# Four-layer graph stack on one core: row sums of layer two partly on VectorE, one more pair of lead in layer three

## The chip, the core and the metric

The kernel runs on one core of one Trainium2 chip. The metric is the device time of one execution in microseconds (us). PE is TensorE, DVE is VectorE, ACT is ScalarE, POOL is GpSimd, SP is the queue that issues most transfers. "L817" is line 817 of the kernel before; in the changed kernel the lines from there on are one lower or a few higher.

## The reference

There are 4096 nodes with 256 features each, and a dense 4096 x 4096 adjacency of zeros and ones. Four layers follow each other; each is attention over the whole graph, masked by the adjacency, then a residual and a layer norm:

```
x = layernorm(x + gat(x))          # layer 1: additive scores, 4 heads
x = layernorm(x + mha(x))          # layer 2: q, k, v with biases, 4 heads of 64
x = layernorm(x + gat1(x))         # layer 3: additive scores, 1 head
x = layernorm(x + cosine(x))       # layer 4: cosine scores

# layer 2
scores = q @ k.T / 8 + (edge.T - 1) * 10000;  ctx = softmax(scores) @ v
# layer 3
h = x @ W;  e = leaky(h @ a[:256] + (h @ a[256:]).T);  out = elu(softmax(where(adj > 0, e, -1e12)) @ h)
```

The sums behind the softmax of layer 2 (the "row sums") are needed for each query and head. Layer 3 needs two dot products for each row of x (source and destination scores). Both are what the change touches.

## The kernel before

All of x stays in SBUF as the tile `X`. Each layer is cut into 8 blocks (`NB`) of 512 query rows. PE, DVE and ACT run in the order in which the program is written ("manual schedule"); POOL and SP are placed by a planner, and each engine works through its own queue in order.

**Layer 2** (`multi_head_attention`). A block has 64 units (`NH`), one for each 64 key rows. Unit j does this:

- `scores`: 4 small products on PE into a PSUM tile `p` (L805), the exponential on ACT in place (L807). There are three buffers of `p`.
- `weights`: DVE multiplies `p` by the mask into `prob` (L817, 128 x 1024 elements). Then `prob` is added to the row sums `den`: for even j by a POOL tensor_tensor into part 0 of `den` (L824), for odd j by a DMA with accumulation that POOL issues, into part 1 or 2 (L830).
- `sums`: 4 products of V and `prob` on PE (L838), three units later (`LAG = 3`).

PE may write the scores of unit j + 3 only when DVE has multiplied unit j. Between the units, `finish(b - 1, j)` does the rest of the block before in small steps: join the parts of `den` (L847, j = 7 and 9), the outputs, the layer norm (L184, j = 35, 37, 39, 41), then `ga.dots` (L501, j = 43, 45, 47, 49), which makes the two dot products of 128 rows for layer 3, then `ga.factors` (j = 51), three exponentials and a small store. `finish` of step j comes after `weights` of unit j + 3, so the first dots follow the multiplication of unit 46.

A dot product is one DVE instruction (tensor_tensor_reduce, in the profile CUSTOM_DVE_ANT_0) that reads 256 elements of `X` and of `a_row`, both in SBUF, and a short one that reads the accumulator.

**Layer 3** (`additive_one`). A block has 16 pairs (`NP`) of 128 key rows. For pair g, `weights` loads a mask of 512 KB (L546, SP), ACT makes `r` (L553, two halves), DVE makes `prob` (L554, two halves) and the first half of `mix` (L434), POOL the second (L435, L436). `sums` does 7 products on PE (L444) two pairs later (`LAG = 2`); the tiles `prob` and `mix` have 3 buffers each, the mask 4. In block 0 there is no `mix`, and `sums` is 4 products (L568); the tail of layer 2 runs between them.

At the end of a block the four PSUM banks `acc` are emptied: `one` on ACT (L449), then five operations on DVE (L450 to L458). The next block's products write these banks. `finish(b - 1, g)` projects (L583, PE), divides and activates (`take`, L589 to L592), adds (`add`, L600, L601) and normalises the block before.

From block 2 on the block b - 2 is also prepared for layer 4 (`Cosine.preparing`, a generator that is moved on one step at chosen g): DVE transposes `y` into `squares` (L127), SP writes `squares` to DRAM (`far`, L131) and reads it back turned (`xT`, L135); then 8 products (L1033), two PSUM banks, with 8 squares on ACT (L1037) written between them; a root (L1040, L159, L160); POOL refines it (L166 to L169); ACT scales (`rows`, L1046); DVE transposes `rows` into a second tile `squares`, POOL writes it to DRAM and reads it back. The two tiles `squares` come from two pools of one buffer each: `gb_squares` and `co_once`.

## Time and profile before

| | us |
|---|---|
| median of 3 runs (lowest to highest) | 2887.21 (2884.02 to 2887.65) |
| the profiled execution, its own time | 2885.52 |
| its span in the profile | 2883.7 |
| TensorE busy in the span | 2798.0 (97%) |
| VectorE, ScalarE, GpSimd busy | 2307.1, 1698.3, 1118.9 |
| granted TensorE clock, mean | 0.997 |

The span is 1.8 us shorter than the execution's own time, and that is 1.7 us under the median. The products of layer 1 end at 724 us of the span, layer 2 runs its units from 812 to 1758 us, layer 3 from there to about 2242 us, layer 4 to the end. In the views below, an instruction's line gives its start, its duration, engine, source line, operation and tiles; in brackets stands the idle time ahead of it and what ended that. A line of waits gives the waiting engine and tile, what it waited for, the total, the number of times and the longest.

### The profile page before, as it was taken

The page shows a single profiled execution, that of the slowest core. Times are in us where ns is not written, and L with a number is a line of the kernel's source. Part 1 is how long each engine was busy: PE and PEld are TensorE (multiplying, and loading weights), DVE is VectorE, ACT ScalarE, POOL GpSimd, SP SyncE. Part 2 cuts the span into 40 slices and gives each one's busy share as a digit, 9 for nine tenths or more (in the row PEclk, how much of TensorE's full clock was granted, in tenths as well). Part 3 has the DMA queues.
Part 4 walks back from the last instruction along what each step waited for, and adds up shares of the span by engine and source line. Part 5 has one row for each costly group of instructions (what it writes and reads, how often), then busy time and mean ns, then how long its engine had stood idle before and what let it go on. Part 6 is the DMA issues. An engine that isn't in the chain of part 4 may idle for free. (4 is left out here: it accounts for less than half of the span.)

```text
span 2883.7 us, 50258 instructions
## 1 busy us (share of the span) xinstructions
PE 2798.0 (97%) x19489; PEld 1427.6 (50%) x19489; DVE 2307.1 (80%) x3010; ACT 1698.3 (59%) x2641; POOL 1118.9 (39%) x1009
## 2 busy tenths in 40 slices
PE   9999999999999999999999998999999999999998
PEld 4333333333543333333333333777877777777776
DVE  8899999998767888788887888777777766666666
ACT  7899999997256655656556564555555422222222
POOL 0010010100068988888888883344445100000000
PEclk9999999999999999999999999999999999999999
DMA  7566667665259989988888987566567544444441
GB/s 207 103 140 138 141 137 148 136 132 92 88 125 193 184 175 161 193 177 180 176 164 187 181 178 178 161 193 199 173 179 212 131 63 63 62 63 60 65 55 34
DMA packets 243666, 405.38 MB, mean 141 GB/s; under 512 B 25201, under 2 KB 125537, under 8 KB 242530
## 3 DMA queue, kind: packets, MB, share of 16 engines
q0 software_dynamic: 103648, 182.48, 40.6%
q1 hardware_dynamic: 133264, 212.45, 24.3%
q10 hardware_dynamic: 6514, 7.23, 0.7%
q8 instruction: 153, 2.51, 0.4%
q14 instruction: 87, 0.71, 0.1%
HBM read 332.27 MB, written 35.73 MB: 128 GB/s over the span
## 5 line engine op out<-in xcount | busy, mean ns | idle before, releaser
L807 ACT ACTIVATE p<-p,shift 128x1024 f32<-128x1024 f32 x512 | 556.2, 1088 | 356.8 <-PE p L805 349.5
L817 DVE TENSOR_TENSOR prob<-p,mask 128x1024 f32<-128x1024 f32 x512 | 620.3, 1221 | 171.7 <-ACT p L807 160.9
L310 PE MATMUL acc<-prob,V 128*32 128x512 f32 x6144 | 664.0, 593 | 1.2 <-DVE prob L300 1.2
L824 POOL TENSOR_TENSOR den<-den,prob 128x1024 f32<-128x1024 f32 x248 | 635.9, 2564 | 51.2 <-DVE prob L817 41.4
L297 ACT ACTIVATE prob<-row,dst 128x512 f32<-128x512 f32 x1020 | 635.0, 712 | 0.6
L300 DVE SCALAR_TENSOR_TENSOR prob<-prob,mask 128x2048 f32<-128x2048 f32 x256 | 580.5, 2287 | 25.7 <-ACT prob L297 25.1
L805 PE MATMUL p<-qT,kT 64*64 64x512 f32 x4096 | 538.7, 592 | 39.6 <-DVE prob L817 39.6
L838 PE MATMUL acc<-prob,V 64*64 64x512 f32 x4096 | 536.8, 589 | 0.0
L310 PEld LDWEIGHTS acc<-prob,V 128*32 128x32 f32 x6144 | 197.3, 110 | 453.0 <-issue 431.6
L444 PE MATMUL acc<-mix,mixed 128*128 128x256 f32 x1440 | 391.4, 381 | 5.7 <-POOL mix L435 4.7
L805 PEld LDWEIGHTS p<-qT,kT 64*64 64x64 f32 x4096 | 153.1, 133 | 325.5 <-issue 237.6
L838 PEld LDWEIGHTS acc<-prob,V 64*64 64x64 f32 x4096 | 157.5, 133 | 285.7 <-issue 278.2
L444 PEld LDWEIGHTS acc<-mix,mixed 128*128 128x128 f32 x1440 | 272.2, 190 | 48.1 <-POOL mix L435 7.9
L1096 DVE TENSOR_TENSOR prob<-prob,mask 128x1024 f32<-128x1024 f32 x128 | 156.5, 1222 | 169.8 <-ACT prob L1088 169.6
L90 POOL COPY tick<-prob 128x1 f32<-128x1 f32 x35 | 38.9, 1112 | 643.3 <-DVE prob L300 642.4
L830 POOL DMA_DIRECT2D den<-prob x240 | 232.7, 969 | 81.4 <-DVE prob L817 59.9
L554 DVE SCALAR_TENSOR_TENSOR prob<-r,own,mask 128x512 f32<-128x512 f32 x256 | 179.7, 743 | 103.7 <-POOL mix L436 42.6
L444 PE MATMUL acc<-prob,X 128*128 128x256 f32 x960 | 251.2, 381 | 10.8 <-DVE quarters L450 9.0
L1021 POOL DMA_DIRECT2D mask<-in_adjT x64 | 47.8, 746 | 521.4 <-DVE prob L1096 418.7
L444 PEld LDWEIGHTS acc<-prob,X 128*128 128x128 f32 x960 | 181.0, 190 | 96.5 <-issue 63.1
L1088 ACT ACTIVATE prob<-p 128x512 f32<-128x512 f32 x144 | 86.0, 598 | 220.8 <-PE p L1084 204.4
L1088 ACT ACTIVATE prob<-g 128x512 f32<-128x512 f32 x112 | 66.7, 596 | 195.5 <-PE g L1084 195.5
(211 smaller groups left out, 2838.3 us busy)
## 6 DMA issues: line engine op xcount, KB each, us to landing
mask<-in_adjT SPq DMA_DIRECT2D x256, 512.0 KB
den<-prob POOLq DMA_DIRECT2D x240, 512.0 KB, 5.3
mask<-edges SPq DMA_DIRECT2D x512, 64.0 KB
mask<-in_adjT POOLq DMA_DIRECT2D x64, 512.0 KB, 5.6
edges<-in_adj POOLq DMA_DIRECT2D x32, 512.0 KB, 9.8
far<-squares SPq DMA_DIRECT2D x16, 512.0 KB
den<-prob SPq DMA_DIRECT2D x16, 512.0 KB
row<-far SPq DMA_DIRECT2D x7, 1024.0 KB
```

The lines of the kernel that those rows point to most:

```text
L297: nc.scalar.activation(z[:, h, :], r, AF.Relu, bias=-1.0, scale=dst[:, j, h:h + 1])
L300: nc.vector.scalar_tensor_tensor(z, z, 1.0, mask[m][:, j % MJ, :].unsqueeze(1).to_broadcast([P, H, QW]), OP.add, OP.mult)
L310: nc.tensor.matmul(acc[b][h * G:(h + 1) * G, n, :], part, prob[b, j][:, h, :], start=(j == 0), stop=(j == NT - 1))
L444: nc.tensor.matmul(acc[at][:, half * HW:(half + 1) * HW], w, a, start=(g == 0 and half == 0), stop=(g == NP - 1), skip_group_check=True)
L554: nc.vector.scalar_tensor_tensor(z[:, n, :], r, ga.own[:, j:j + 1], mask[:, n, :], OP.add, OP.mult)
L805: nc.tensor.matmul(p[c * d:(c + 1) * d, r, :], kT[half, c, at:at + d], qT[half, c, cols], start=True, stop=True)
L807: nc.scalar.activation(p, p, AF.Exp, bias=shift)
L817: nc.vector.tensor_tensor(z, p, mask[m][:, j % MJ, :].unsqueeze(1).to_broadcast([P, KC, QW]), OP.mult)
L824: nc.gpsimd.tensor_tensor(to, to, flat, OP.add)
L830: nc.gpsimd.dma_start(to, flat, accum_op=OP.add)
L838: nc.tensor.matmul(acc[b][c][r * d:(r + 1) * d, :], V[half, j, r * d:(r + 1) * d], prob[b, j][half, r, :], start=(j == 0), stop=(j == NH - 1))
L1096: nc.vector.tensor_tensor(z, z, co.mask[b, 2 * g // MJ][:, lo:lo + 2, :], OP.mult)
```

## The change

Layer 2: in the blocks 1 to 7, the additions of units 44, 48, 52 and 56 to part 0 of `den` go from POOL to DVE (28 of 248 POOL additions). The dots move to the steps right behind these, so that DVE's order there is multiplication, addition, two dot products. `factors` moves from step 51 to 57, the load of the first row for layer 3 from step 57 of block 0 to step 63 of block 1.

Layer 3: `LAG` goes from 2 to 3, `prob` and `mix` get 4 buffers, the mask 3. The first `squares` shares the one buffer of the second. `finish` and the preparation are laid out anew over g; in the preparation the 8 products come first, and the 8 squares follow in two later steps.

Layer 4 takes the two added steps of the preparation up in its own list.

```diff
@@ additive_one
-            mp = pool(lay, "gb_mask", 4)
-            zp = pool(lay, "gb_z", 3)
+            mp = pool(lay, "gb_mask", 3)
+            zp = pool(lay, "gb_z", 4)
...
-            sq = pool(lay, "gb_squares", 1)
             far = pool(lay, "gb_far", 2, space=bass.MemoryType.DRAM)
-            follow.turning = xp, sq, far
+            follow.turning = xp, None, far
...
             def finish(b, g):
+                if g in (1, 3, 5, 7):
+                    project(bank, b, g // 2)
                 if g in (2, 4, 6, 8):
-                    project(bank, b, g // 2 - 1)
+                    take(sb, b, g // 2 - 1)
                 if g in (3, 5, 7, 9):
-                    take(sb, b, g // 2 - 1)
-                if g in (4, 6, 8, 10):
-                    add(b, g // 2 - 2)
+                    add(b, g // 2 - 1)
+                elif g == 10:
+                    roots[b] = begin_root(mvs[b])
                 elif g == 11:
-                    roots[b] = begin_root(mvs[b])
-                elif g == 12:
                     v, r, n = roots[b]
                     end_root(v, r, n, nc.gpsimd)
...
-                elif g in (13, 14):
+                elif g in (12, 13):
                     v, r, _ = roots[b]
-                    for k in (2 * g - 26, 2 * g - 25):
+                    for k in (2 * g - 24, 2 * g - 23):
...
-                elif g == 15:
+                elif g == 14:
...
-            LAG = 2
+            LAG = 3
...
-                        if b > 1 and g in (3, 5, 10, 11, 12, 13, 14, 15):
+                        if b > 1 and g in (0, 2, 8, 9, 10, 11, 12, 13, 14, 15):
                             follow.prepare(bank, b - 2, 1)
@@ multi_head_attention, weights
                     else:
-                        nc.gpsimd.tensor_tensor(to, to, flat, OP.add)
+                        eng = nc.vector if b and j in relief else nc.gpsimd
+                        eng.tensor_tensor(to, to, flat, OP.add)
@@ multi_head_attention, finish
-                elif j in (43, 45, 47, 49):
-                    ga.dots(b * QB + (j - 43) // 2)
-                elif j == 51:
+                if j + LAG in relief:
+                    ga.dots(b * QB + relief.index(j + LAG))
+                elif j == 57:
                     ga.factors(b)
-                elif j == 57 and b == 0:
-                    ga.row(b, nc.sync)
+                elif j == 63 and b == 1:
+                    ga.row(0, nc.sync)
...
             LAG = 3
+            relief = (44, 48, 52, 56)
@@ Cosine.preparing
-            xT = yield from block_turning(*self.turning, rows, nc.sync)
+            turned, squares, far = self.turning
+            xT = yield from block_turning(turned, squares or self.once, far, rows, nc.sync)
...
                     nc.tensor.matmul(prs[k // 2][:, k % 2, :, :], xT[:, c, k], w_sb[:, c, :],
                                      start=(c == 0), stop=(c == KC - 1))
+            for k in range(QB):
+                if k % 2 == 0:
+                    yield
                 for n in range(2):
                     sq = in_.tile([P, P], FP, name="sq")
                     nc.scalar.activation(sq, prs[k // 2][:, k % 2, n, :], AF.Square, accum_out=norm[:, k, n:n + 1])
@@ cosine_attention
-            steps = {(0, j + n): (NB - 2 + b, step) for b, j in enumerate((1, 12)) for n, step in ((0, 3), (4, 1), (5, 1), (7, 1), (8, 3))}
+            steps = {(0, j + n): (NB - 2 + b, step) for b, j in enumerate((1, 12)) for n, step in ((0, 3), (4, 3), (5, 1), (7, 1), (8, 3))}
```

## The prediction

> **What bounds the kernel now.** I read the busy shares first: PE is busy for 97% of the span, and the mean granted clock is 0.997. A change that moves no PE work can only win back the idle time of PE, so I next asked what PE waits for in layer 2 (window 825 to 1745) and layer 3 (1745 to 2250).

> ```profile
> PE 2798.0 (97%) x19489; PEld 1427.6 (50%) x19489; DVE 2307.1 (80%) x3010; ACT 1698.3 (59%) x2641; POOL 1118.9 (39%) x1009
> ...
> PE p L805 <- DVE prob L817: 38.8, 28, 2.0
> ...
> PE g L1033 <- ACT sq L1037: 9.3, 12, 1.1
> PE acc L444 <- DVE quarters L450: 9.0, 6, 1.7
> PE acc L444 <- POOL mix L435: 4.7, 8, 0.8
> ```

> The second line is all that PE loses in layer 2: 28 waits, which is 7 blocks of 4. The others belong to layer 3. The timeline around the first dots of block 1 (DVE, then POOL, then PE) shows where the 28 come from, and the last two lines show the same dots later, in layer 3:

> ```profile
> 1004.93 1.23 DVE L817 TENSOR_TENSOR prob<-p,mask 128x1024 f32<-128x1024 f32 x1 [0.56 <-ACT p L807]
> 1006.07 0.42 DVE L501 CUSTOM_DVE_ANT_0 neg<-X,a_row 128x256 f32<-128x256 f32 x1
> 1006.41 0.08 DVE L501 DVE_READ_ACCUMULATOR2_ANT dot<- 128x1 f32 x1
> 1006.53 2.73 DVE L501 CUSTOM_DVE_ANT_0 neg<-X,a_row 128x256 f32<-128x256 f32 x1
> 1009.19 0.08 DVE L501 DVE_READ_ACCUMULATOR2_ANT dot<- 128x1 f32 x1
> 1009.19 2.35 DVE L817 TENSOR_TENSOR prob<-p,mask 128x1024 f32<-128x1024 f32 x2
> ...
> 1006.31 2.66 POOL L824 TENSOR_TENSOR den<-den,prob 128x1024 f32<-128x1024 f32 x1
> ...
> 1010.46 1.09 PE L805 MATMUL p<-qT,kT 64*64 64x512 f32 x8 [0.78 <-DVE prob L817]
> ...
> 1015.56 1.09 PE L805 MATMUL p<-qT,kT 64*64 64x512 f32 x8 [1.44 <-DVE prob L817]
> ...
> 1791.50 0.43 DVE L501 CUSTOM_DVE_ANT_0 neg<-X,a_row 128x256 f32<-128x256 f32 x1
> 1791.97 0.42 DVE L501 CUSTOM_DVE_ANT_0 neg<-X,a_row 128x256 f32<-128x256 f32 x1
> ```

> The first dot takes 0.42. Then POOL starts its addition (1006.31 to 1008.97), and the second dot takes 2.73 and ends with it. In layer 3, where POOL adds nothing, all eight dots take 0.42 or 0.43. A dot costs 0.42 alone and lasts until POOL is done beside an addition.

> **Layer 2: what is removed.** PE starts units 1.72 us apart. The product after the first dots starts at 1010.46 instead of 1009.50, 0.96 late; each of the next three comes 1.62 late (DVE takes 5.10 for two units that PE makes in 3.43). A block loses 0.96 + 3 x 1.62 = 5.82, seven blocks 40.7 us.

> **Layer 2: what is added.** I take slack from the same place. Normally DVE has 0.56 of idle time per unit. Between multiplications 46 and 47 stood 3.12 us of dots, so DVE came 3.12 - 0.56 = 2.56 late and PE 0.96: some 1.6 us of lateness is free. Now DVE's insert at unit 48 is the addition, 1.14 from start to start (the nearest row is L847, the same form, 1216 ns in each of 14 executions, beside busy POOL), and two dots with their reads, 0.46 each: 2.06. That is 1.50 late, nothing lost. But the addition reads `den`, so it must wait for POOL's addition of unit 46. POOL starts 0.28 after the multiplication of 46 and takes 2.35; DVE, catching up, has multiplied 48 only 2.35 after 46. That makes a wait of about 0.35, a lateness of 1.85, a loss of 0.25. At unit 44 a scaled row (L184, 0.34) joins: 0.25 to 0.5. A block loses 1.0 to 1.2, seven blocks 7.7 us. Bounds: nothing, if POOL always keeps up; 15 us, twice that, since POOL's additions beside transfers reach 3.1 (block 5 runs 0.9 behind). Net for layer 2: -33 (-41 to -26).

> Everything queued behind the waiting addition on DVE is the two dots and multiplication 45, 49 and so on; PE waits for that, which is what I priced. POOL's next addition (46, 50) waits for DVE's, but also for a later multiplication, so costs nothing. POOL is freed of 28 x 2.56 = 72 us; its idle time there is not on the path. `factors` moves to where no dot is queued before it (ACT waited 1.6 us for the last dot), and the row load moves along SP with half a layer in hand: both nothing.

> [...]

> **Layer 3.** Per block, PE's waits between 2061.85 and 2124.30 are 0.71 + 0.77 (products behind squares on the same banks), 0.78 (`mix`) and 0.37 + 1.69 + 0.20 at the end, where DVE is late:

> ```profile
> 2121.34 1.40 DVE L554 SCALAR_TENSOR_TENSOR prob<-r,own,mask 128x512 f32<-128x512 f32 x2
> 2122.78 0.87 DVE L434 TENSOR_TENSOR mix<-prob 128x512 f32<-128x512 f32 x1
> 2123.57 0.68 DVE L450 TENSOR_TENSOR quarters<-one,acc 128x512 f32<-128x512 f32 x1
> ...
> 2121.91 0.70 PE L444 MATMUL acc<-prob,X 128*128 128x256 f32 x2 [0.37 <-ACT one L449]
> 2124.30 0.70 PE L444 MATMUL acc<-prob,X 128*128 128x256 f32 x2 [1.69 <-DVE quarters L450]
> ```

> With the products ahead of the squares, the 1.48 go. The third pair of lead covers the 0.78. But the end gets later. I follow DVE from the pair after the last `take` (pair 12, DVE at 2099.93 before) to the emptying of the banks. Before, it takes 23.6 us (L450 at 2123.57). After, I add the rows up: pair 13 at +4.0 (no squares ahead of it); 14 at +8.5, since ACT must do one root (0.35) and four squares (1.1) before `r`; 15 at +12.1; 16 at +16.6, behind eight scalings (2.17); the transposes of `rows`; 17 at +19.9. Then comes the new wait: the transpose of `y` needs the shared `squares`, which POOL still writes to DRAM. POOL issues that after `mix` of pair 16, at about +20.2, and before it took 3.7 (2119.82 to 2123.5), so the transpose starts at +23.9, 2 us late; pair 18 follows at +25.2, L450 at +27.2. Queued behind it on DVE are pair 18 and the emptying, and PE waits for the latter. The transpose, though, stood behind the emptying before, so that pair 3 of the next block comes at +29.7 in both. From there to the next pair 12 it is 31.5 after (take and add pairs, 7.85 for two) and 32.7 before. A block takes about 61.2 instead of 61.4 to 62.4: -0.7 each for five blocks, -3.5. The last block has neither the shared tile's wait nor a block behind it and keeps its 1.88 + 0.70: -2.6. At the start, the joins of the row sums go behind a fourth pair, whose mask is issued only after the first pair (1762.84): +1.5, between 0 and 3. In the middle of a block a mask has two pairs (6 us) to land; the nearest row, POOL's mask, lands in 5.6, so nothing. Net: -4. Bounds: the chain after pair 12 may be all hidden (five blocks of 1.48 + 0.78 + 1.3, where 1.3 is 2.26 less the 0.96 that the undisturbed end of block 1 costs, and the last block: -20), or the transfer lands 2 to 3 us later than in my row (five times: +12).

> **Sum.** Against the profiled execution: 2885.5 - 33 - 4 = 2848.5. That execution is 1.7 under the median of the runs, so I say 2850.

> **Rivals.** (1) Layer 3 comes clean: the lead hides the shared tile. For it: POOL's transfer could land sooner. Against: the wait stands ahead of the emptying in DVE's order. Time: 2885.5 - 33 - 20 + 1.7 = 2834. (2) Layer 3 loses: the same wait, longer, since transfers are busy there (0.65 of the engines). Time: 2885.5 - 33 + 12 + 1.7 = 2866. (3) Slower: POOL lags behind DVE by a pair, and each moved addition waits for it. POOL is nearly full in layer 2 (45 of 50 us), and an addition with its issue takes 2.56 + 0.97. A wait of 3.5 makes 2.06 + 3.5 - 0.56 - 1.6 = 3.4 lost at each of 28, 95 us in all: 2885.5 - 40.7 + 95 - 4 + 1.7 = 2937. It decides from a wait of some 1.7 us on: (40.7 + 4) / 28 = 1.6 lost at each, and 0.1 that the slack takes. Against: POOL starts that addition 0.15 to 0.6 us after its multiplication in six blocks, 0.96 in block 5. (4) The change doesn't do what it says: the dots still last 2.45 for another reason, such as POOL's issues. Then 2.0 more is lost at each, 28 x 2.0 = 56: 2885.5 - 40.7 + 56 - 4 + 1.7 = 2898. Against: one dot beside an issue alone took 0.61.

> **How the numbers follow.** My forecast has 0.57, rival 1 0.15, rival 2 0.20, rivals 3 and 4 together 0.04; 0.04 is for gain and loss cancelling, within 0.2% (5.8 us, about what this kernel's measurement can tell from none). So faster 0.92, same 0.04, slower 0.04. The range goes from rival 1 to rival 2 with the bounds of layer 2 partly added: 2832 to 2869.

> **What would show it.** In layer 2: all dots at 0.42, PE's wait for L817 from 38.8 to under 15, blocks of about 114.6 us instead of 119.3 (the first scores of block 1 start at 920.74, of block 7 at 1636.40). In layer 3: no wait of PE for the squares or `mix`, a DVE wait for a POOL transfer ahead of L127, PE's wait for L450 grown to some 4 us per block. Dots of over 1 us, or additions on DVE preceded by over 1.5 us of idle time, would prove me wrong.

## The result and the profile after

| us | before | after |
|---|---|---|
| median of 16 runs on one chip | 2886.84 | 2893.90 |
| lowest to highest | 2884.02 to 2890.03 | 2886.74 to 2901.31 |
| the profiled execution (its span) | 2885.52 (2883.7) | 2892.32 (2890.5) |
| mean granted TensorE clock | 0.997 | 0.987 |

One run of after (5999.05 us) was disturbed as a whole and is left out of the range; the median of the other 15 is 2893.70. The ratio of after to before is 1.0026, 95% interval 1.0018 to 1.0034: the changed kernel is 0.26% **slower**. The forecast was 2850 (2832 to 2869), so it missed by 44 us, and its sign was wrong.

First the page of after, its span and busy shares:

```profile
span 2890.5 us, 50162 instructions
PE 2803.9 (97%) x19489; PEld 1440.2 (50%) x19489; DVE 2276.5 (79%) x3038; ACT 1694.1 (59%) x2641; POOL 1049.3 (36%) x981
```

DVE and POOL have less to do, as meant, but PE is busy for 6 us longer with the same 19489 products: some of them ran at a lower clock (mean granted 0.987 instead of 0.997). The waits of PE in layer 2 (window 825 to 1745; a line that belongs to layer 3 is left out) show that the stated aim was reached, and that something else came in:

```profile
...
PE acc L838 <- ACT kept L843: 6.8, 4, 2.9
PE p L804 <- DVE prob L816: 3.2, 5, 1.1
PE acc L838 <- issue: 2.1, 1, 2.1
```

The 38.8 us of waits for the multiplication are down to 3.2. New are waits for `kept` (the copy of a finished block's sums out of PSUM), at the changeover from one block to the next. The waits of PE in layer 3 (window 1720 to 2260):

```profile
PE acc L444 <- DVE quarters L450: 37.0, 6, 8.1
PE acc L567 <- DVE prob L553: 8.5, 1, 8.5
PE g L1035 <- ACT h L591: 4.4, 6, 1.0
PE g L860 <- DVE den L847: 2.2, 1, 2.2
```

The waits for the squares (9.3) and for `mix` (4.7) are gone; the wait for the emptying went from 9.0 to 37.0.

I cut the span at four instants that both traces have: first and last scores of layer 2 (L804), the emptying (L450) of block 1 of layer 3, of block 6, of block 7. The same cuts serve for all experiments.

| us of the span | before | after | difference | forecast |
|---|---|---|---|---|
| layer 2, first to last scores | 942.3 | 915.5 | -26.8 | -33 |
| start of layer 3, to the emptying of block 1 | 122.2 | 133.0 | +10.8 | +1.5 |
| blocks 2 to 6 of layer 3 | 308.1 | 332.0 | +23.9 | -3.5 |
| last block of layer 3 | 58.2 | 56.9 | -1.3 | -2.6 |
| everything else | 1452.9 | 1453.1 | +0.2 | 0 |

So the gain of layer 2 came (a fifth short) and layer 3 took it away, and more. Three places had to be explained: the 6 us short in layer 2, the 9 us too many at the start of layer 3, and the 27 us in its blocks.

**The blocks of layer 3.** DVE, then PE, at the end of block 5 in the trace of after (start, duration, engine, line, operation, tiles, in brackets the idle time ahead and what ended it):

```profile
2050.16 1.30 DVE L127 STREAM_TRANSPOSE squares<-rows 128x512 f32<-128x512 f32 x2
2051.38 1.37 DVE L553 SCALAR_TENSOR_TENSOR prob<-r,own,mask 128x512 f32<-128x512 f32 x2
...
2057.16 1.30 DVE L127 STREAM_TRANSPOSE squares<-y 128x512 f32<-128x512 f32 x2 [3.69 <-DMA far<-squares]
2058.39 1.37 DVE L553 SCALAR_TENSOR_TENSOR prob<-r,own,mask 128x512 f32<-128x512 f32 x2
...
2060.40 0.68 DVE L450 TENSOR_TENSOR quarters<-one,acc 128x512 f32<-128x512 f32 x1
```

```profile
2053.97 0.70 PE L444 MATMUL acc<-prob,X 128*128 128x256 f32 x2 [0.69 <-ACT one L449]
2061.14 1.22 PE L444 MATMUL acc<-prob,X 128*128 128x256 f32 x2 [6.47 <-DVE quarters L450]
2062.16 1.91 PE L444 MATMUL acc<-mix,mixed 128*128 128x256 f32 x4
2063.86 1.06 PE L444 MATMUL acc<-mix,X 128*128 128x256 f32 x2
...
2069.04 0.59 PE L444 MATMUL acc<-mix,mixed 128*128 128x256 f32 x2
```

The transposition of `y` waits 3.69 for POOL's transfer out of the one `squares` tile; a pair and the emptying stand behind it, so PE idles 6.47. And then the products take 1.06 for 0.59: after this wait the records show a granted clock of 0.50 from 2057.1 to 2067.3. The same follows each of the six block ends, for 3.4, 10.2, 6.8, 10.2, 6.8 and 6.8 us. The first of these, of block 1, where POOL has no transfer out of `squares` under way yet, stands behind a wait of 2.57 us; the others stand behind waits of 6.5 to 8.1.

**The end of layer 2.** The waits for `kept` led to a place where no instruction is busy. This is the view of the transfers of after from 1376 to 1390, in 40 slices of 0.35 us: the busy tenths of the 16 DMA engines, GB/s, and one queue's packets, MB and share:

```profile
DMA  6999900000359999794000002866498999999999
GB/s 151 164 253 221 211 13 0 0 0 0 6 97 165 148 94 39 12 35 12 0 0 0 0 0 41 64 61 82 101 192 178 218 218 212 263 203 237 243 282 209
...
q10 hardware_dynamic: 528, 0.00, 2.1%
```

Queue 10 is the store of `factors` (`far<-src`, L514): 512 pieces of 4 bytes, issued at 1374.1 and moved at 1376.3 to 1376.7. Hardly anything is moved from 1377.8 to 1379.8 and from 1381.3 to 1384.4. Packet by packet, 4 KB pieces of the additions to `den` that take 0.33 us otherwise then take up to 5.25. In layer 2 such packets (4 KB or less, over 1 us) come in one bunch per block, apart from a few single ones; each bunch begins 1.7 to 4.2 us behind the first of this store's packets, in before and after alike (122 and 150 of the 30,720 packets of 4 KB). The change moved the store, with `factors`, from step 51 to 57, that is from unit 54 to unit 60 of the block. Before, the last packet of the last bunch ended at 1749.6, and the first masks of layer 3 were issued at 1755.3. After, the packets of that bunch start from 1729.0 to 1736.6, and the masks are issued at 1728.4. DVE at the start of layer 3 in after:

```profile
1739.44 1.41 DVE L553 SCALAR_TENSOR_TENSOR prob<-r,own,mask 128x512 f32<-128x512 f32 x2 [6.80 <-DMA mask<-in_adjT]
...
1747.15 1.41 DVE L553 SCALAR_TENSOR_TENSOR prob<-r,own,mask 128x512 f32<-128x512 f32 x2 [4.66 <-DMA mask<-in_adjT]
```

The first mask is used 11.1 us after its issue; before it was 6.1 (1755.32 to 1761.41).

### The profile page after: what moved, and what is told of

Its sections match the earlier page's. It is cut to its first block, busy times and chain, and to the rows that moved or that the text cites. A ratio compares the mean times of both kernels' runs of the same rounds, so it can differ in the third digit from the quotient of the medians.

```text
span 2890.5 us, 50162 instructions
## 1 busy us (share of the span) xinstructions
PE 2803.9 (97%) x19489; PEld 1440.2 (50%) x19489; DVE 2276.5 (79%) x3038; ACT 1694.1 (59%) x2641; POOL 1049.3 (36%) x981
## 5 line engine op out<-in xcount | busy, mean ns | idle before, releaser
L300 DVE SCALAR_TENSOR_TENSOR prob<-prob,mask 128x2048 f32<-128x2048 f32 x256 | 580.3, 2285 | 25.8 <-ACT prob L297 25.2
L824 POOL TENSOR_TENSOR den<-den,prob 128x1024 f32<-128x1024 f32 x220 | 560.9, 2549 | 41.2 <-DVE prob L816 33.0
L804 PE MATMUL p<-qT,kT 64*64 64x512 f32 x4096 | 535.0, 592 | 4.7 <-DVE prob L816 4.0
L444 PE MATMUL acc<-mix,mixed 128*128 128x256 f32 x1440 | 395.7, 384 | 0.7 <-DVE quarters L577 0.7
L444 PEld LDWEIGHTS acc<-mix,mixed 128*128 128x128 f32 x1440 | 277.4, 193 | 40.1 <-issue 1.0
L804 PEld LDWEIGHTS p<-qT,kT 64*64 64x64 f32 x4096 | 152.9, 133 | 287.1 <-issue 233.7
L444 PE MATMUL acc<-prob,X 128*128 128x256 f32 x960 | 253.9, 384 | 38.9 <-DVE quarters L450 37.0
L830 POOL DMA_DIRECT2D den<-prob x240 | 228.0, 950 | 137.6 <-DVE prob L816 92.9
L444 PEld LDWEIGHTS acc<-prob,X 128*128 128x128 f32 x960 | 182.7, 192 | 125.2 <-issue 63.1
```

The costliest lines, as they stand in the source:

```text
L300: nc.vector.scalar_tensor_tensor(z, z, 1.0, mask[m][:, j % MJ, :].unsqueeze(1).to_broadcast([P, H, QW]), OP.add, OP.mult)
L444: nc.tensor.matmul(acc[at][:, half * HW:(half + 1) * HW], w, a, start=(g == 0 and half == 0), stop=(g == NP - 1), skip_group_check=True)
L804: nc.tensor.matmul(p[c * d:(c + 1) * d, r, :], kT[half, c, at:at + d], qT[half, c, cols], start=True, stop=True)
L824: eng.tensor_tensor(to, to, flat, OP.add)
L830: nc.gpsimd.dma_start(to, flat, accum_op=OP.add)
```

## The experiments

Every ratio is to the kernel before, run beside it. The last four columns are the cuts of the table above. Line numbers in a view are those of the run's own kernel, and the code of the edits is abridged.

| run | median, us | ratio (95% interval) | layer 2 | start | blocks 2 to 6 | last |
|---|---|---|---|---|---|---|
| before (profile) | | | 942.3 | 122.2 | 308.1 | 58.2 |
| after (profile) | 2893.90 | 1.0026 (1.0018 to 1.0034) | 915.5 | 133.0 | 332.0 | 56.9 |
| l2_only | 2868.44 | 0.9928 (0.9913 to 0.9943) | 924.2 | 128.2 | 308.0 | 57.8 |
| l3_only | 2914.51 | 1.0087 (1.0072 to 1.0102) | 944.2 | 129.1 | 328.0 | 57.1 |
| turn_late | 2875.55 | 0.9950 (0.9936 to 0.9965) | 920.9 | 133.2 | 307.9 | 60.0 |
| own_squares | 2872.47 | 0.9950 (0.9933 to 0.9966) | 918.6 | 133.4 | 308.2 | 56.8 |
| l2_odd | 2894.40 | 1.0032 (1.0022 to 1.0041) | 945.5 | 126.6 | 308.5 | 58.0 |
| own_squares_odd | 2900.82 | 1.0052 (1.0037 to 1.0067) | 947.7 | 131.6 | 307.7 | 56.8 |
| l2_products_first | 2857.26 | 0.9901 (0.9886 to 0.9916) | 914.4 | 128.0 | 303.1 | 56.3 |
| l2_odd_products_first | 2885.92 | 0.9999 (0.9990 to 1.0008) | 948.4 | 126.2 | 300.8 | 57.4 |
| l2_store_late | 2883.71 | 0.9995 (0.9986 to 1.0004) | 936.6 | 127.5 | 307.6 | 57.8 |
| l2_early | 2852.66 | 0.9882 (0.9866 to 0.9899) | 907.5 | 125.2 | 308.9 | 59.4 |
| l2_early_products_first | 2844.51 | 0.9858 (0.9843 to 0.9872) | 907.2 | 125.8 | 301.1 | 56.6 |
| after_early | 2873.97 | 0.9960 (0.9945 to 0.9975) | 906.6 | 127.6 | 328.7 | 57.3 |
| after_wide_store | 2868.33 | 0.9934 (0.9919 to 0.9949) | 900.5 | 126.1 | 330.4 | 56.5 |
| after_early_own | 2854.90 | 0.9884 (0.9868 to 0.9901) | 907.2 | 128.4 | 307.6 | 56.9 |
| turned_store | 2839.32 | 0.9836 (0.9819 to 0.9852) | 905.5 | 120.9 | 301.9 | 56.3 |
| turned_store_sp | 2835.29 | 0.9819 (0.9805 to 0.9834) | 901.0 | 123.8 | 300.8 | 56.3 |

The theory at this point: layer 2's part is a gain of some 27 us, the layer-3 part loses some 24 us by the shared `squares`, and the slow start of layer 3 comes from layer 2's transfers. The rivals: the longer lead itself is the loss, or the two parts only hurt together.

### The two halves of the change, each alone

l2_only is the kernel before with the edits of `multi_head_attention` alone; l3_only is after without them.

> The kernel before with the layer-2 part of the change alone (additions of units 44, 48, 52, 56 on VectorE, dots behind them). My theory (layer 2 gains 27 us as in the trace of after, and the 10.8 us that the start of layer 3 lost come from this part, since the transfers that accumulate den lag at the end of the faster layer 2): time 11 to 18 us below before, first mask of layer 3 again some 11 us after its issue. Rival A (the start of layer 3 lost its 10.8 us to the three mask buffers and the fourth pair of lead): 24 to 29 us below before, first mask some 6 us after its issue.

> The kernel after with the layer-2 part undone, so the layer-3 part alone. My theory: the blocks 2 to 6 of layer 3 lose some 24 us, the last gains 1.3, the start is nearly unchanged: 20 to 26 us above before. Rival A (the start's loss belongs to this part): 31 to 36 us above before. Rival B (the two parts hurt each other, neither does alone): within 5 us of before.

The parts are nearly additive: -0.72% and +0.87%, together +0.15%, against +0.26% measured. l3_only lies 25.6 us above before (20 to 26 expected), l2_only 20.5 below, between what theory and rival said. At the start of layer 3 both were half right: l2_only loses 6.0 there, l3_only 6.9.

### The shared squares

```
turn_late:    elif g == 14: ... far_y store
-                 follow.prepare(bank, b, 1, ys[b])
+             elif g == 15: follow.prepare(bank, b, 1, ys[b])
own_squares:  sq = pool(lay, "gb_squares", 1); follow.turning = xp, sq, far
              co_mask bufs=4 -> 3
```

> The kernel after with the transposition of y moved from step 14 back behind the emptying of the banks (step 15), still into the shared buffer. My theory (the wait for the shared squares, and the half clock after PE's long wait, are paid because the transposition stands ahead of the emptying in VectorE's order): PE's wait for the emptying falls from 6.2 to 2 to 3 us a block, the half clock goes, blocks 2 to 6 from 66.3 to about 62 us: 18 to 24 us below after. Rival (the longer lead itself makes the chain to the emptying long, with a pair more ahead of it): the wait stays above 5 us, time within 6 us of after.

> The kernel after with a buffer of its own for the first squares, paid with one of the four mask buffers of layer 4 (4 to 3). The transposition stays ahead of the emptying, but waits for no transfer. My theory: the wait of 3.7 us goes, PE's wait for the emptying falls from 6.2 to about 2.5 to 3.5 us a block (the transposition itself, 2.6, stays ahead of the emptying), blocks 2 to 6 at 62 to 63 us: 15 to 22 us below after, unless layer 4 pays for its third mask buffer. Rival (it is the order and the lead, not the shared buffer): the wait stays above 5 us and the time within 6 us of after.

Both give blocks 2 to 6 their old 308 us back: 24 us for an edit of place, 24 for a buffer. DVE, then PE, at the same block end in own_squares:

```profile
2046.73 1.30 DVE L127 STREAM_TRANSPOSE squares<-y 128x512 f32<-128x512 f32 x2
...
2049.96 0.68 DVE L450 TENSOR_TENSOR quarters<-one,acc 128x512 f32<-128x512 f32 x1
```

```profile
2050.70 1.22 PE L444 MATMUL acc<-prob,X 128*128 128x256 f32 x2 [2.70 <-DVE quarters L450]
```

The same order and the same lead, but no wait ahead of the transposition: PE idles 2.70 instead of 6.47. The rival falls; by the ratios both are 0.76% (22 us) below after. But neither is better than before in these blocks. What the waits for squares and `mix` gave back, new ones take: PE waits 16.1 us for the emptying in own_squares (9.0 before), and 12.6 us for `h` in turn_late. In own_squares the granted clock is still 0.50 for 3.4 us behind each of the six block ends.

### A wrong turn: fewer transfers

At this point I took the transfers of `den` themselves for the reason of the late block ends (the engines are busy to 0.92 in layer 2), and gave POOL four of them per block to add.

```
-                    if j < 4:
+                    if b and j - 1 in relief:
+                        nc.gpsimd.tensor_tensor(den[b][:, 0, :], den[b][:, 0, :], flat, OP.add)
+                    elif j < 4:
```

> The layer-2 part alone, and GpSimd, which it freed of four additions a block, adds the units 45, 49, 53 and 57 of blocks 1 to 7 itself, in place of 28 of the 224 accumulating transfers of these blocks. My theory (the faster layer 2 now meets the transfers of den: VectorE's multiplication waits for a transfer that still reads its prob buffer, 17 to 25 us in all, and the first masks of layer 3 queue behind them): these waits fall under 8 us, PE's waits for kept (10.1 us) under 4, layer 2 from 924 to 912 to 917 us, the first mask of layer 3 lands in 6 to 9 us instead of 12: time 8 to 15 us below the layer-2 part alone. Rival (the limit is not the transfers but the order on VectorE and ScalarE at the end of a block): layer 2 within 3 us of 924, PE's waits for kept stay.

> The kernel after with its own squares buffer (three mask buffers in layer 4), and GpSimd adding the units 45, 49, 53 and 57. My theory: the same 8 to 15 us below the kernel with own squares alone, all in layer 2 and at the start of layer 3; layer 3's blocks unchanged at 61.3 us. Rival: within 4 us of it.

Both miss: layer 2 loses 21 and 29 us. DVE, then POOL, in l2_odd:

```profile
1011.04 1.23 DVE L825 TENSOR_TENSOR den<-den,prob 128x1024 f32<-128x1024 f32 x1 [1.35 <-POOL den L825]
```

```profile
1006.22 2.35 POOL L829 TENSOR_TENSOR den<-den,prob 128x1024 f32<-128x1024 f32 x1 [2.82 <-DVE prob L817]
1008.65 2.35 POOL L825 TENSOR_TENSOR den<-den,prob 128x1024 f32<-128x1024 f32 x1
```

POOL now makes two additions between two of DVE's, and DVE's waits 1.35 for the second. The next ones stand at 1019.13 and 1027.23, so four units take 8.09 instead of 4 x 1.715 = 6.86. The DMA engines' share fell from 0.90 to 0.93 to 0.74 to 0.83, yet DVE waited 34.7 us for transfers that still read its `prob` (24.6 in l2_only): fewer transfers alone did not take these waits away.

### Products ahead of squares, without the rest of the layer-3 part

```
+            for k in range(QB):
                 for n in range(2):
                     sq = in_.tile([P, P], FP, name="sq")
```

> The layer-2 part alone, and in the preparation of layer 4 the eight products ahead of the eight squares (order alone, no further steps, lead of two pairs, own squares). My theory: of the change's layer-3 part only this is worth anything here; PE's 9.5 us of waits for the squares go, ScalarE does the squares in one go some 1.3 us later: 5 to 9 us below the layer-2 part alone. Rival (the squares in one go hold up r and so VectorE, and the wait comes back for mix or for the emptying): within 3 us.

> Both of the edits before on the layer-2 part. If they are independent, their gains add up: 14 to 23 us below the layer-2 part alone, 34 to 44 us below before.

The order alone saves 4.9 and 7.7 us in blocks 2 to 6 and 0.6 to 1.5 in the last; by the ratios l2_products_first is 0.27% (7.8 us) below l2_only, as expected. The sum that l2_odd_products_first should show was wrong because the l2_odd half was.

### The store of factors

```
l2_store_late:  +   elif j == 20 and b: ga.store(b - 1)     # blocks 0 to 5
l2_early, after_early:
-            relief = (44, 48, 52, 56)       +            relief = (40, 44, 48, 52)
-                elif j == 57:               +                if j == 51:
                     ga.factors(b)
```

> The layer-2 part alone, with one store moved: in the first six of seven blocks the small store of factors (512 elements of 4 bytes) goes from step 57 to step 20 of the next block; the seventh stays at step 57 of the last block. My theory (some 4 us after each of these stores the packets of all transfers take 1 to 5 us instead of 0.33, for 5 to 8 us; since the change put the store at unit 60 this falls on the end of the block, where den and kept change over, and the seventh on the first masks of layer 3): the stalls follow the store to the middle of the blocks, PE's waits for kept fall from 10 us to under 3, layer 2 from 924 to 913 to 919 us, but the start of layer 3 stays late (74 us from the last scores to the first emptying, as in the layer-2 part alone): 5 to 11 us below the layer-2 part alone. Rival (the store is innocent, the transfers of den lag because layer 2 runs faster): waits for kept stay, within 3 us.

> The layer-2 part alone, with the additions on VectorE and the dots four units earlier (40, 44, 48, 52) and factors with its store back at step 51, where it was before the change. My theory: the stalls fall at unit 56 to 60, as before; PE's waits for kept fall under 3 us, layer 2 to 910 to 915 us (a loss of 0.3 to 1 us a block at the scaled rows, which now join three dots), and the last store no longer meets the first masks, so that the first emptying comes 68 to 70 us after the last scores instead of 74: 12 to 18 us below the layer-2 part alone, 32 to 38 us below before. Rival (the store is innocent): within 4 us of the layer-2 part alone.

> The same, with the eight products ahead of the eight squares in the preparation of layer 4 (lead of two pairs as before). Both gains should add up: 8 to 11 us below the kernel with the early store alone, 40 to 48 us below before.

> The kernel after with the additions, the dots and factors four to six units earlier as above; its layer 3 unchanged. My theory: layer 2 gains 2 to 6 us and the start of layer 3 some 3 to 6 us (a part of its 10.8 us belongs to the fourth pair of lead); blocks 2 to 6 of layer 3 stay at 65.6 to 67.2 us: 6 to 12 us below after, so a little below before instead of above. Rival (the store is innocent): within 3 us of after.

With the store back at step 51 no wait for `kept` is left, layer 2 takes 907 us, and the start loses 3 instead of 6: by the ratios l2_early is 0.46% (13 us) below l2_only, as expected, with products first another 8 in the same session, and after_early 0.66% (19 us) below after (more than the 6 to 12 I expected: 9 in layer 2, 5 at the start, 3 in the blocks). l2_store_late missed: by the ratios it is 0.67% (19 us) above l2_only, not 5 to 11 us below. The bunches of slow packets followed the store to the middle of the blocks (they start from 1434.2 to 1440.6 in block 5), and no wait of PE for `kept` is left in its layer 2, both as the theory says. But there they put POOL behind, whose next transfer in block 5 waits 6.58 us for an earlier one, and the first addition on DVE, at unit 44, waits for POOL; PE then waits 26.7 us in all for the multiplications. The waits of DVE in its layer 2:

```profile
DVE den L830 <- POOL den L830: 18.8, 7, 4.8
```

Of the three places tried, step 51 costs least: no addition on DVE comes soon after it there, and the block's end is still some units away.

### Is it the 4-byte pieces?

```
after_wide_store:  far = self.far.tile([P, QB]); nc.scalar.dma_start(far, src)   # 128 pieces of 16 bytes
turned_store:      nc.vector.transpose(self.turned, self.wide)                   # 32 x 32 blocks
                   for p in range(0, P, 32): nc.scalar.dma_start(far[:, p:p + 32], self.turned[p:p + QB, :])
turned_store_sp:   the same from nc.sync
```

> The kernel after with one change: the store of factors writes its 512 values as 128 pieces of 16 bytes instead of 512 of 4, at the same step 57. The values come out in another order, so this leaves out the right order of the query factors of layer 3 (the amount of work is the same). My theory, if the many 4-byte pieces cause the stall of the transfers: packets of over 1 us vanish behind the store, PE's waits for kept go, layer 2 from 915 to 906 to 910 us, first emptying of layer 3 72 us after the last scores instead of 77: 8 to 16 us below after. Rival 1 (any store of this queue there does it, or what is read back): stalls and time unchanged, within 4 us. Rival 2 (the stall grows with the pieces): stalls of 1 to 2 us instead of 5 to 8, 4 to 12 us below after.

> The kernel after with both causes taken away: additions, dots and factors at the earlier units, and a buffer of its own for the first squares (three mask buffers in layer 4). If the two are independent, the gains add up: some 18 us (early) and 20 us (own squares), so 34 to 42 us below after, 27 to 35 us below before; layer 2 at 907 us, blocks 2 to 6 of layer 3 at 61 to 62 us. Rival (they share a cause): less than 28 us below after.

The view of the transfers in after_wide_store, 1371 to 1385, the same place of the block (the store's 128 pieces and 16 others at 1371.6):

```profile
DMA  4998920269999899999997699999999999938999
...
q10 hardware_dynamic: 144, 0.00, 0.6%
```

The short dip right behind the store is left (1372.8 to 1373.8), but the long stop is gone: in the whole of layer 2 one 4 KB packet of 30,720 takes over 1 us, and layer 2 takes 900.5: 41.8 less than before, and more than I had expected (by the ratios the run is 0.92%, 27 us, below after). Of PE's waits in layer 2 (825 to 1745; the other lines belong to layer 3) this is left:

```profile
...
PE p L804 <- DVE prob L816: 1.1, 3, 0.5
```

Same step, same queue, same number of bytes: the 512 pieces of 4 bytes are what stops the transfers. Whether it is their size or their number, no run separates. With both causes taken away after_early_own takes 2854.90, with 907.2 in layer 2 and 307.6 in the blocks, 33 us below before by its ratio of 0.9884. That is near the 37 us of the forecast, though the start is still 6.2 us longer than before.

The order of the 16-byte store is not the one that layer 3 needs, so DVE turned the factors first.

> The layer-2 part alone (additions at 44 to 56, factors at step 57), products ahead of squares, lead of two pairs; and VectorE turns the 512 factors in blocks of 32 x 32 first, so that the store is four transfers of four pieces of 128 bytes from ScalarE's queue, in the right order. My theory (the 4-byte pieces cause the stall): no stall behind the store, layer 2 at 900 to 904 us as with the pieces of 16 bytes, the first emptying of layer 3 68 to 71 us after the last scores, layer 3 as with products first: 2833 to 2842 us, 16 to 24 us below the same kernel with the 4-byte store (2857). Rival (four issues on ScalarE, 0.4 us each, make the exponential late by 1.2 us, or the 16-byte result had another reason): above 2850.

> The same with the four transfers issued from SP's queue instead of ScalarE's. My theory: within 4 us of the one before, since neither queue sets the pace; ScalarE saves 1.2 us once a block, SP issues them behind masks that wait for their buffers.

Both come out near what was expected: 2839.32 lies within its range, with layer 2 at 905.5 (1.5 us above its own) and the start at 120.9; the version from SP's queue is 4.0 us faster, at the edge of its 4, with 901.0 and 123.8. The page of turned_store_sp, and its waits of PE in layer 2 (825 to 1745; the other lines of that answer belong to layer 3):

```profile
span 2833.0 us, 50187 instructions
PE 2788.9 (98%) x19489; PEld 1426.4 (50%) x19489; DVE 2279.1 (80%) x3047; ACT 1696.5 (60%) x2641; POOL 1053.9 (37%) x981
```

```profile
...
PE p L810 <- DVE prob L822: 1.6, 3, 0.9
```

This version, layer 2's part of the change, the turned store and the products ahead of the squares with the old lead of two, beats both kernels: 1.8% below before. Its four runs lie within 0.7 us of each other, where those of l2_only spread over 6.5.

## Why the prediction was wrong

**Layer 2, what is removed (40.7): right.** All dots take 0.42 or 0.43, also beside the moved additions, as DVE shows in after:

```profile
1368.42 1.23 DVE L824 TENSOR_TENSOR den<-den,prob 128x1024 f32<-128x1024 f32 x1
1369.56 0.42 DVE L501 CUSTOM_DVE_ANT_0 neg<-X,a_row 128x256 f32<-128x256 f32 x1
...
1370.02 0.42 DVE L501 CUSTOM_DVE_ANT_0 neg<-X,a_row 128x256 f32<-128x256 f32 x1
```

Without the slow packets layer 2 gained 41.8. The addition takes 1.23 in all 28 cases and is not held up by POOL, which issues at most a transfer beside it (L830) and makes no addition. What it would take with an addition of POOL's already under way, as nearly all second dots of before had it (they took 2.45 to 3.16), is not shown. My row for its price was not quite what I said: of the 14 executions of L847 in before, 12 stand beside an addition on POOL. They kept their 1.22, but there DVE had started first, by 0.24 or 0.58 us, and POOL's addition took 3.20 or 2.86 instead of 2.35.

**Layer 2, what is added (7.7): too high.** PE lost 3.2 in after, 1.1 in after_wide_store; DVE's additions waited 1.4 us for POOL in all of after. The size of the slack was right: l2_odd, with a wait of 1.35, lost 1.23 per addition where my sum gives 2.06 + 1.35 - 0.56 - 1.6 = 1.25. That is the mechanism of rival 3, and in l2_odd and l2_store_late it decided.

**"`factors` moves ...: nothing": the failed step of layer 2.** I priced ACT's wait for the last dot and forgot the store that the step issues, though the same store was in the trace of before, with a stop of the transfers behind it. At step 51 it had cover, nine units (15 us) to the block's end; at step 57 there were three. There the 4-byte store cost layer 2 some 15 us (915.5 against 900.5 in after_wide_store; after_early, with the store back at step 51 and the additions and dots moved too, takes 906.6) and the start of layer 3 some 5 to 7 (133.0 against 126.1 and 127.6). That this came out as a shortfall of only 6 in layer 2 is luck: the 7.7 that I had subtracted were not needed.

**Layer 3, the chain to the emptying: the failed step, in two terms.** The order of events was as told: the wait stood where I put it, ahead of L127, and the squares' and `mix` waits went. In the block that ends at 2060.40, counted from pair 12 (2030.84), DVE came 0.6 to 0.9 late at pairs 13 to 17 (20.5 instead of 19.9 for pair 17), the transposition at 26.3 instead of 23.9, the emptying at 29.6 instead of 27.2. The mis-sized term is POOL's transfer: issued at 2051.87, landed at about 2057.1, so 5.3 instead of the 3.7 of my row. The missing term is the clock. PE's waits account for some 15 of the 23.9 us: (37.0 - 9.0 - 9.3 - 4.7 + 4.4) x 5/6. The remaining 9 are products at half clock, an estimate by the records: of each stretch at 0.50, some 3.4 to 6.2 us lie in products, and half of that is lost (behind the wait above, pairs of products start 0.86 us apart instead of 0.43), about 12 in five blocks against 1.6 before. I had asked what each wait costs, and not what PE runs at after it. The waits of 6.5 to 8.1 us in after have 6.8 or 10.2 us at half clock behind them, but shorter ones did it too: in own_squares 2.70, soon after another idle stretch of 0.67, was followed by 3.4 us at half clock, and even 1.69, soon after 0.38, was at one of the five ends of blocks 2 to 6 in before (at 2061.5). The last block, which gained 1.3 instead of 2.6, has a part of it too: the stretch at 0.50 behind block 6 lasts until 2197.0, 4.2 us into it.

**The start (+1.5): too low.** Half of the 10.8 or more is the store; l3_only, with the store still at step 51, loses 6.9 there, and after_wide_store 3.9. The clock has a part in it too: it is granted at 0.50 for 13.7 us of the start in after, for 6.8 us in before and in after_wide_store. That the joins behind the fourth pair cost time I had seen coming, but not how much: PE waits 4.4 us for them in l3_only (L859). How the rest divides between three masks and the lead I did not take apart.

**The rivals.** Rival 2 named the right mechanism for the loss (the transfer lands later, +12) at half of its size. That both costs would come together was in no case of mine.

## What to carry to other kernels

When a step is moved, price every transfer that it issues at its new place, however small (here 2 KB cost layer 2 some 15 us): ask which large transfers are under way there and who waits for them. The buffer that was shared here to make room turned into a wait of 3.69 us for the transfer that empties it; before sharing, see what stands behind the waiting instruction. And a wait of PE can cost more than its length, as here (6.47 us at the end of block 5, and 10.2 us with a granted clock of 0.50 around its end): look at the granted clock behind it, and count the products that ran at half speed.
